# Two heads' scores emptied together: one maximum or one exponential over two PSUM banks

## The chip, the cores and the metric

The kernel runs on one core of a Trainium2 chip. A core has TensorE (matrix products), VectorE and ScalarE (both can read the results of TensorE), GpSimd, and SyncE, which here only issues DMAs. TensorE writes into PSUM: 128 partitions of eight banks, and a bank holds 512 fp32 numbers per partition. Before a bank can be written anew, whoever reads it must have finished.

The metric is the device time of one execution in microseconds. In the profile, PE is TensorE's matrix products, PEld its weight loads (they run beside the products), DVE is VectorE, ACT is ScalarE, POOL is GpSimd and SP is SyncE.

## The reference, cut to what matters

Two layers in a row work on `x` of 2 x 1024 tokens with 256 columns. Each has self-attention with 16 heads of 16 columns, then cross-attention to a context of 64 tokens, then a feed-forward part; in the first layer this is a mixture of eight experts of which each token uses two. The change touches self-attention alone:

```python
q, k, v = heads(q_in, wq, bq), heads(kv_in, wk, bk), heads(kv_in, wv, bv)   # 2 x 16 x 1024 x 16
scores = jnp.einsum('bhqd,bhkd->bhqk', q, k) / jnp.sqrt(jnp.float32(dh))    # 1024 x 1024 per head
attn = jax.nn.softmax(scores, axis=-1)
out = jnp.einsum('bhqk,bhkd->bhqd', attn, v)
```

The softmax needs, for each query, the largest score over 1,024 keys, the exponentials of the scores less that maximum, and their sum.

## The kernel before, in words

All of PSUM is one tile, `banks`, of 128 x 8 x 512. A Python list `free` holds the numbers of the banks that are not promised to anybody, and is worked while the program is written, not while it runs. `bank()` (L260) takes the bank at the head of the list. Whoever takes a bank gives it back to the end of the list as soon as the instruction that empties it has been written down. A bank at the head may therefore still be being read when the program runs; the first matmul that writes it then waits for its reader. Four engines (PE, DVE, ACT, SP) run their instructions in exactly the order in which the code writes them.

Self-attention (`self_attention`, from L556) handles four heads at a time. A *cell* is four heads (j = 0 to 3), 512 queries and 128 keys; a layer has 128 cells, eight to a group of heads. Each cell's scores are computed twice, in two kinds of tiles of 128 x 512, one bank each:

- kind "a", ten cells ahead (`LEAD`): queries in the partitions, 512 keys in the columns. It is two matmuls (the high and low parts of the queries), and VectorE empties it by a maximum over its columns (L911) into `mx`.
- kind "b", for the cell itself: 128 keys in the partitions, 512 queries in the columns. It is three matmuls, of which the third subtracts the maxima (`QB`), and ScalarE empties it by an exponential (L921) into `pt`, a tile of the pool tag "p1" with 12 buffers.

`scores` (L926) writes one cell's tiles. It has four lanes, one per head; a lane uses its own 32 rows of TensorE. In one *wave* each lane writes one matmul. Lanes 0 and 1 have first their "b" tile and then their "a" tile; lanes 2 and 3 the other way round. So waves 1 to 2 finish the "a" tiles of heads 2 and 3, wave 3 the "b" tiles of heads 0 and 1, and wave 5 the other four. Banks are taken at the first wave of a tile: four in wave 1, two in wave 3, two in wave 4. After wave 3, and at the end, the banks of the finished tiles go back to the list, the later finished half and the earlier one in turn (L955). After a full cell the list therefore reads b0 a2 b1 a3 b2 a0 b3 a1, where each bank is named by the tile that it last held.

The main loop (L1100) writes, cell by cell: the scores; at the end of a group `collect` (L968: the maxima over both halves of the keys, laid out for the transposes of `largest`, L804); every second cell, or sometimes for one cell by itself, `product` (L988), which multiplies the exponentials of one or two *earlier* cells by the values (L997, one bank), copies the result out of PSUM on ScalarE (L1006, L1009) and lets GpSimd add it up (L1010); and then a few microseconds of other work which a planner (`Stream`, L141) picks by costs and due times: projections of the next heads (L669: product, split on ScalarE L660 and VectorE L661, DMA), values (L633), cross-attention (L1265, L1304, L1357), and more. All of these take their banks with `bank()`, one or two at a time. The planner's costs don't depend on which banks are free, so the order of the instructions doesn't either. Before the first cell of a layer, ten cells of "a" tiles alone are written (`early`, L959). The last ten cells of a layer hold "b" tiles alone.

The two lines that empty the tiles before:

```python
nc.vector.tensor_reduce(to, sc, AX.X, ALU.max)             # L911: 128 x 512 -> 128 x 1
nc.scalar.activation(pt, sc, AF.Exp, scale=SCALE)          # L921: 128 x 512 -> 128 x 512
```

Of the kernel before, what the change touches and what calls it, by code (L numbers as in the profile page):

```python
# [41 lines left out]
F32 = mybir.dt.float32  # L42
F32R = mybir.dt.float32r
I32 = mybir.dt.int32
U32 = mybir.dt.uint32
AF = mybir.ActivationFunctionType
ALU = mybir.AluOpType
AX = mybir.AxisListType
# [3 lines left out]
P = 128  # L52
# [5 lines left out]
SCALE = 0.25  # L58
# [12 lines left out]
NK = 5  # L71
# [160 lines left out]
def two_blocks(  # L232
# [16 lines left out]
    nc = tc.nc  # L249
# [7 lines left out]
    banks = psum.tile([P, 8, 512], F32, tag="banks", name="banks")  # L257
    free = list(range(8))

    def bank():  # L260


        i = free.pop(0)
        return i, banks[:, i, :]


    x_sb = const.tile([P, NT, D], F32, name="x_sb")
# [41 lines left out]
    ones = const.tile([P, P], F32, name="ones")  # L309
# [236 lines left out]
    def make_heads(pool, layer):  # L546


        KS = [pool.tile([P, S], F32R, name=f"KS{layer}{i}") for i in range(NK)]
        QS = [  # L550
            [pool.tile([P, 512], F32R, name=f"QS{layer}{i}{part}") for part in "hl"]
            for i in range(4)
        ]
        return KS, QS

    def self_attention(layer, tail, heads, arrive, extra, when_ready, beside=None):  # L556
# [6 lines left out]
        names = f"s{layer}"  # L563
        pools = ExitStack()

        def results_pool():
            side = {"side": "right"} if layer else {}
            return tail.enter_context(tc.tile_pool(name=f"opool{layer}", bufs=2, **side))

        def weights_pool():  # L570
            return pools.enter_context(tc.tile_pool(name=f"qpool{layer}", bufs=1, side="right"))
# [7 lines left out]
        if layer == 0:  # L579
            qpool = spool = weights_pool()  # L580
        else:
            spool = pools.enter_context(tc.tile_pool(name="spool", bufs=1))
        KS, QS = heads or make_heads(qpool, layer)
# [14 lines left out]
        QB, mx = {}, {}  # L598
        exps = {}
        now = [-99]  # L600
        reduced = [None]
# [16 lines left out]
        def norm():  # L618
            yield from norm_task(TB, TB, ln, x_turned(1), f"{names}1", held=held[0])
            if layer == 0:  # L620
                add_bias(TB, TB, bias_out[0])
# [166 lines left out]
        def add_heads(b, qh, pair):  # L788
# [3 lines left out]
            if qh == 0:  # L792
                stream.add(
                    keys(b, pair), 3.44, last=last, mark=("K", h),
                    after=[("norm", b)], rank=1,
# [3 lines left out]
        def need_heads(h):  # L799
            if h % 8 in (0, 2) and h > 0:  # L800
                stream.until(("K", h))
            stream.until(("Q", h))
# [92 lines left out]
        def score(kind, cell, j):  # L895

            h, n = divmod(cell, 8)
            b, g = h // 8, h % 4
            K = KS[(4 * b + g) % NK]
            r = slice(32 * j, 32 * j + 32)  # L900
            if kind == "a":
                qc, kh = divmod(n, 2)
                if h not in mx:
                    mx[h] = small.tile([P, 4, 4, 2], F32, tag="mx", name=f"mx_{names}{h}", bufs=3)
                to = mx[h][:, qc, j, kh : kh + 1]
                products = [
                    (q[r, qc * P : (qc + 1) * P], K[r, kh * 512 : (kh + 1) * 512]) for q in QS[h % 4]
                ]

                def reduce(sc):  # L910
                    nc.vector.tensor_reduce(to, sc, AX.X, ALU.max)  # L911
                    return True

                return products, reduce
            products = [(K[r, n * P : (n + 1) * P], q[r, :]) for q in QS[h % 4]]
            r = slice(32 * j, 32 * j + 2)
            products.append((ones[r, :].bitcast(F32R), QB[h][r, :]))

            def drain(sc):
                pt = qpool.tile([P, 512], F32, tag="p1", name=f"pt_{names}{cell}{j}", bufs=12)  # L920
                nc.scalar.activation(pt, sc, AF.Exp, scale=SCALE)  # L921
                exps[cell, j] = pt

            return products, drain

        def scores(lanes):  # L926

            lanes = [[score(*t) for t in lane] for lane in lanes]
            at = [[0, None] for _ in lanes]
            emptied, wave = [], 0  # L930
            while any(lanes):
                done = []
                for lane, now in zip(lanes, at):
                    if not lane:
                        continue
                    products, drain = lane[0]
                    if now[1] is None:
                        now[1] = bank()
                    i, sc = now[1]
                    lhsT, rhs = products[now[0]]  # L940
                    now[0] += 1
                    last = now[0] == len(products)
                    nc.tensor.matmul(sc, lhsT=lhsT, rhs=rhs, start=now[0] == 1, stop=last)  # L943
                    if last:
                        done.append((drain, i, sc))
                        lane.pop(0)
                        now[:] = 0, None
                for drain, i, sc in done:
                    if drain(sc):
                        reduced[0] = i  # L950
                emptied.extend(i for _, i, _ in done)
                wave += 1
                if wave == 3 or not any(lanes):
                    half = len(emptied) // 2
                    for pair in zip(emptied[half:], emptied[:half]):  # L955
                        free.extend(pair)
                    emptied = []

        def early(cell):  # L959

            h, n = divmod(cell, 8)
            if h not in mx:
                mx[h] = small.tile([P, 4, 4, 2], F32, tag="mx", name=f"mx_{names}{h}", bufs=3)
            for c in (cell, cell + 1):
                scores([[("a", c, j)] for j in range(4)])
                yield 0.9

        def collect(h):  # L968
# [87 lines left out]
        else:  # L1056
# [3 lines left out]
            opool, qpool = results_pool(), weights_pool()  # L1060
# [3 lines left out]
        if layer == 1:  # L1064
            stream.made.update([("K", 2), ("Q", 2)])
        for qh, pair in ((0, 1), (1, 0), (1, 1))[layer:]:
# [6 lines left out]
            norm(), 4.0, last=64 - LEAD - 16, mark=("norm", 1), light=True,  # L1073
            after=["measured", ("K", 2), ("Q", 6), ("values", 0, TB - 1)],
        )
# [4 lines left out]
        if layer == 0:  # L1080
# [3 lines left out]
            for ahead in range(0, LEAD, 2):  # L1084
                cell = now[0] = ahead - LEAD
# [14 lines left out]
        for cell in range(ncell + 2):  # L1100
            now[0] = cell
            ahead = cell + LEAD
            if ahead < ncell and ahead % 16 == 0:
                need_heads(ahead // 8)
            has_a, has_b = ahead < ncell, cell < ncell
            maxima[0] = has_a
            lanes = []
            for j in range(4):
                tiles = [("b", cell, j)] * has_b + [("a", ahead, j)] * has_a
                lanes.append(tiles[::-1] if j > 1 else tiles)  # L1110
            scores(lanes)
            if ahead % 8 == 7 and has_a:
                h = ahead // 8
                collect(h)
                stream.add(
                    largest(h), 0.75, first=cell + 1, last=cell + 2, mark=("QB", h), rank=99, light=True
                )
            if (cell + 1) % 8 == 0 and cell + 1 < ncell:
                stream.until(("QB", (cell + 1) // 8))
            for go in later.pop(cell, []):  # L1120
                go()
            if cell >= 2 and cell % 2 == 0:
                product([c for c in (cell - 2, cell - 1) if c not in alone])
            if has_a:
                most = 2.2 - stream.steady(cell, 1.1)
                while cell % 2 == 1 and most > 0.9:
                    cost = stream.step(cell, heavy=True)
                    if cost is None:
                        break
                    most -= cost  # L1130
            else:
                owed = min(owed, 3.0) + max(stream.pace(cell), 2.0)
                if cell % 2 == 0 and owed < 2.5:
                    continue
                most = 2.2
                while owed > 0.5 and most > 0.0:
                    cost = stream.step(cell)
                    if cost is None:
                        break
                    owed -= cost  # L1140
                    most -= cost

            if cell % 2 == 1 and most > 1.2 and cell < ncell:
                alone.add(cell - 1)
                product([cell - 1])
# [989 lines left out]
    def block(layer, tail, heads=None, beside=None):  # L2135
# [75 lines left out]
        def around(*begin):  # L2211
            beside(*begin)
            open_pools()

        stream, later = self_attention(layer, tail, heads, arrive, extra, when_ready, around)
        return stream, later, made, ready

# [12 lines left out]
    stream, later, _, _ = block(0, tail)  # L2230
# [217 lines left out]
```

## Time and profile before

| what | us |
|---|---|
| median of 3 runs | 1542.13 (1539.37 to 1545.07) |
| the profiled execution, its own time | 1547.58 |
| its span, first to last instruction | 1545.8 |
| cells with both kinds of scores, layer 0 | from 66 to 511 |
| the mixture of experts, between the layers | from 511 to 918 |
| cells with both kinds of scores, layer 1 | from 918 to 1345 |
| the last cells and the forward part | from 1345 to 1546 |

Busy time in the stretches that the change touches, and in the whole span (us):

| stretch | PE | PEld | DVE | ACT | POOL |
|---|---|---|---|---|---|
| 66 to 511 | 418.10 | 196.86 | 361.21 | 345.41 | 169.81 |
| 918 to 1345 | 406.65 | 196.62 | 353.08 | 344.74 | 173.16 |
| span | 1444.7 | 840.9 | 1005.8 | 938.7 | 442.7 |

The mean granted clock of TensorE was 0.977. In the page's groups of instructions a row reads: line, engine, operation, output and input, shapes, count; then busy time and the mean length of one in ns; then how long the engine had been idle before them and what ended most of it. In the list of waits a row gives who waited for whom, the total in us, how often, and the longest. In the timeline a row gives start and length in us, engine, line and operation, where neighbouring instructions of one group are merged (x4), and in brackets the idle time before. The chain goes back from the last instruction to whatever released it, piece by piece.

### The profile page before, as it was taken

The page shows a single profiled execution, that of the slowest core. Times are in us where ns is not written, and L with a number is a line of the kernel's source. Part 1 is how long each engine was busy: PE and PEld are TensorE (multiplying, and loading weights), DVE is VectorE, ACT ScalarE, POOL GpSimd, SP SyncE. Part 2 cuts the span into 40 slices and gives each one's busy share as a digit, 9 for nine tenths or more (in the row PEclk, how much of TensorE's full clock was granted, in tenths as well). Part 3 has the DMA queues.
Part 4 walks back from the last instruction along what each step waited for, and adds up shares of the span by engine and source line. Part 5 has one row for each costly group of instructions (what it writes and reads, how often), then busy time and mean ns, then how long its engine had stood idle before and what let it go on. Part 6 is the DMA issues. An engine that isn't in the chain of part 4 may idle for free. (4 is left out here: it accounts for less than half of the span.)

```text
span 1545.8 us, 29995 instructions
## 1 busy us (share of the span) xinstructions
PE 1444.7 (93%) x11220; PEld 840.9 (54%) x11220; DVE 1005.8 (65%) x2219; ACT 938.7 (61%) x1845; POOL 442.7 (29%) x582
## 2 busy tenths in 40 slices
PE   6899999999989987899999999999999999999998
PEld 3443344444445454688888674435444444456666
DVE  6787788889787657541115668977788888844400
ACT  3287787887877834333224347977788788863321
POOL 1142133444553121131112014311265365401010
PEclk9799999999989998999999999999999999999999
DMA  4444641111110021666566542122211112000000
GB/s 158 148 176 162 225 153 49 49 43 36 35 50 15 16 81 41 200 224 235 183 204 234 167 159 76 50 97 76 77 57 35 37 42 80 22 8 29 8 14 27
DMA packets 65605, 146.09 MB, mean 95 GB/s; under 512 B 10570, under 2 KB 24140, under 8 KB 65068
## 3 DMA queue, kind: packets, MB, share of 16 engines
q1 hardware_dynamic: 62236, 135.24, 25.8%
q0 software_dynamic: 3216, 8.85, 1.5%
q8 instruction: 91, 1.49, 0.4%
q14 instruction: 62, 0.51, 0.1%
HBM read 91.96 MB, written 51.86 MB: 93 GB/s over the span
## 5 line engine op out<-in xcount | busy, mean ns | idle before, releaser
L911 DVE TENSOR_REDUCE mx_s<-banks 128x1 f32<-128x512 f32 x1024 | 634.5, 682 | 110.2 <-PE banks L943 109.4
L921 ACT ACTIVATE pt_s<-banks 128x512 f32<-128x512 f32 x1024 | 534.2, 604 | 123.8 <-PE banks L943 117.4
L1010 POOL TENSOR_TENSOR acc_s<-acc_s,part_s 128x512 f32<-128x512 f32 x138 | 176.7, 1281 | 350.3 <-ACT part_s L1009 349.3
L997 PE MATMUL banks<-pt_s,v_s 128*18 128x512 f32 x2048 | 264.5, 611 | 13.1 <-ACT pt_s L921 8.3
L943 PE MATMUL banks<-qb_s,ones 2*128 2x512 f32 x1024 | 203.3, 396 | 0.0
L1947 PE MATMUL banks<-w_slot,h_s 128*128 128x256 f32 x560 | 125.2, 380 | 1.5 <-issue 1.1
L997 PEld LDWEIGHTS banks<-pt_s,v_s 128*18 128x18 f32 x2048 | 42.9, 97 | 132.5 <-ACT pt_s L921 74.7
L1947 PEld LDWEIGHTS banks<-w_slot,h_s 128*128 128x128 f32 x560 | 105.4, 190 | 17.2 <-issue 1.7
L1009 ACT COPY part_s<-banks 128x512 f32<-128x512 f32 x151 | 90.9, 602 | 34.8 <-PE banks L997 33.8
L1956 DVE SCALAR_TENSOR_TENSOR ys<-banks,gate,b 128x256 f32<-128x256 f32 x35 | 16.9, 484 | 136.0 <-PE banks L1947 136.0
L943 PEld LDWEIGHTS banks<-qb_s,ones 2*128 2x128 f32 x1024 | 98.1, 187 | 9.0
L1962 POOL DMA_INDIRECT results<-ys,to x35 | 33.9, 968 | 225.3 <-DVE ys L1956 169.2
L1922 ACT ACTIVATE h_s<-banks,w_slot 128x256 f32<-128x256 f32 (+1 forms) x104 | 41.0, 445 | 92.9 <-issue 53.9
L1916 PE MATMUL banks<-xsT,w_slot 128*128 128x256 f32 (+1 forms) x416 | 85.1, 357 | 0.9 <-ACT xsT L406 0.9
L1916 PEld LDWEIGHTS banks<-xsT,w_slot 128*128 128x128 f32 x416 | 70.9, 190 | 12.0 <-issue 2.8
L2112 PE MATMUL banks<-w_ff,h_f 128*128 128x256 f32 x256 | 57.0, 379 | 0.0
L2103 ACT ACTIVATE h_f<-banks,w_ff 128x512 f32<-128x512 f32 x32 | 21.9, 687 | 56.9 <-PE banks L2100 56.9
L2100 PE MATMUL banks<-hT_f,w_ff 128*128 128x512 f32 x128 | 56.3, 593 | 0.0
L673 PE MATMUL banks<-xT_s,w_att 128*128 128x512 f32 x104 | 51.5, 620 | 2.9 <-ACT pt_s L921 2.2
L1631 POOL DMA_INDIRECT sorted_rows<-xd_m,at_m x32 | 31.2, 976 | 75.4 <-DVE at_m L1623 43.5
L2112 PEld LDWEIGHTS banks<-w_ff,h_f 128*128 128x128 f32 x256 | 48.1, 190 | 7.6 <-issue 1.4
L1922 ACT ACTIVATE h_s<-banks,spare 128x256 f32<-128x256 f32 (+1 forms) x56 | 21.7, 443 | 48.2 <-PE banks L1916 35.6
(371 smaller groups left out, 3064.1 us busy)
## 6 DMA issues: line engine op xcount, KB each, us to landing
w_slot<-in_ff_w_dram SPq DMA_DIRECT2D x40, 576.0 KB
sorted_rows<-fill SPq DMA_DIRECT2D x36, 520.0 KB
w_slot<-in_ff_w_dram SPq DMA_DIRECT2D x26, 514.0 KB
whole<-acc_s SPq DMA_DIRECT2D x30, 256.0 KB
spare<-in_ff_w_dram SPq DMA_DIRECT2D x14, 514.0 KB
q_parts<-spare SPq DMA_DIRECT2D x13, 512.0 KB
KS<-k_parts SPq DMA_DIRECT2D x12, 512.0 KB
k_parts<-spare SPq DMA_DIRECT2D x10, 512.0 KB
```

The lines of the kernel that those rows point to most:

```text
L673: nc.tensor.matmul(p, lhsT=w[:, at + k * D + pair * P : at + k * D + (pair + 1) * P], rhs=xT[b][:, k, blk * 512 : (blk + 1) * 512], start= ...
L911: nc.vector.tensor_reduce(to, sc, AX.X, ALU.max)
L921: nc.scalar.activation(pt, sc, AF.Exp, scale=SCALE)
L943: nc.tensor.matmul(sc, lhsT=lhsT, rhs=rhs, start=now[0] == 1, stop=last)
L997: nc.tensor.matmul(o[32 * j : 32 * j + VW, :], lhsT=V[b][:, cell % 8, 4 * g + j, :], rhs=exps.pop((cell, j)), start=(cell == cells[0]), st ...
L1009: nc.scalar.copy(part, o)
L1010: helper().tensor_tensor(acc[h], acc[h], part, ALU.add)
L1916: nc.tensor.matmul(ph[:, n, :], lhsT=w[:, at : at + P], rhs=xT[:, k, :], start=(k == 0), stop=(k == 1),)
L1922: nc.scalar.activation(h1[:, f, :rows], ph[:, n, :], AF.Gelu, bias=w[:, W_B1 + f : W_B1 + f + 1])
L1947: nc.tensor.matmul(py, lhsT=h1[:, f, h * P : (h + 1) * P], rhs=w[:, f * D : (f + 1) * D], start=(f == 0), stop=(f == 7),)
L2100: nc.tensor.matmul(ph, lhsT=w1[:, at : at + P], rhs=hT[:, k, :], start=(k == 0), stop=(k == 1))
L2112: nc.tensor.matmul(py[:, n, :], lhsT=h1[:, f, t * P : (t + 1) * P], rhs=w2[:, f * D : (f + 1) * D], start=(f == 0), stop=(f == 7),)
```

## The change

Heads 0 and 1 make one pair of lanes, heads 2 and 3 the other. A pair takes two banks at once with the new `two_banks()`: two banks (2k, 2k+1) that lie side by side, both in the list, and among such pairs the one whose later member stands nearest to the head; if there is none, the first two banks of the list. Both tiles of a pair are then emptied by one instruction over 1,024 columns: a maximum of 128 x 2 x 512 into two numbers per partition, or an exponential of 128 x 2 x 512 into one `pt` of 128 x 2 x 512 (six buffers in place of twelve of half the size). Where the two banks do not lie side by side, two instructions are used as before. The order of the matmuls is unchanged. The banks go back to the list pair by pair, after wave 3 and at the end, so that after a full cell the list reads b0 b1 a2 a3 b2 b3 a0 a1.

`bank()`, for all other work, no longer takes simply the head. It looks at the first four of the list and takes the first whose neighbour is not in the list at all, or is among its last three; if there is none, the head.

```diff
--- before.py
+++ after.py
@@ -259,9 +259,19 @@
 
     def bank():
 
-
-        i = free.pop(0)
+        late = free[-3:]
+        i = next((i for i in free[:4] if i ^ 1 not in free or i ^ 1 in late), free[0])
+        free.remove(i)
         return i, banks[:, i, :]
+
+    def two_banks():
+
+        pairs = [(max(map(free.index, (i, i + 1))), i) for i in range(0, 8, 2) if {i, i + 1} <= {*free}]
+        i = min(pairs)[1] if pairs else None
+        got = (i, i + 1) if pairs else free[:2]
+        for i in got:
+            free.remove(i)
+        return [(i, banks[:, i, :]) for i in got]
 
 
     x_sb = const.tile([P, NT, D], F32, name="x_sb")
@@ -895,65 +905,74 @@
         def score(kind, cell, j):
 
             h, n = divmod(cell, 8)
-            b, g = h // 8, h % 4
-            K = KS[(4 * b + g) % NK]
+            g = h % 4
+            K = KS[(4 * (h // 8) + g) % NK]
             r = slice(32 * j, 32 * j + 32)
+            if kind == "a":
+                qc, kh = divmod(n, 2)
+                return [
+                    (q[r, qc * P : (qc + 1) * P], K[r, kh * 512 : (kh + 1) * 512]) for q in QS[h % 4]
+                ]
+            products = [(K[r, n * P : (n + 1) * P], q[r, :]) for q in QS[h % 4]]
+            r = slice(32 * j, 32 * j + 2)
+            return [*products, (ones[r, :].bitcast(F32R), QB[h][r, :])]
+
+        def drain(kind, cell, j, i):
+
+            h, n = divmod(cell, 8)
+            two = i[1] == i[0] + 1
             if kind == "a":
                 qc, kh = divmod(n, 2)
                 if h not in mx:
                     mx[h] = small.tile([P, 4, 4, 2], F32, tag="mx", name=f"mx_{names}{h}", bufs=3)
-                to = mx[h][:, qc, j, kh : kh + 1]
-                products = [
-                    (q[r, qc * P : (qc + 1) * P], K[r, kh * 512 : (kh + 1) * 512]) for q in QS[h % 4]
-                ]
-
-                def reduce(sc):
-                    nc.vector.tensor_reduce(to, sc, AX.X, ALU.max)
-                    return True
-
-                return products, reduce
-            products = [(K[r, n * P : (n + 1) * P], q[r, :]) for q in QS[h % 4]]
-            r = slice(32 * j, 32 * j + 2)
-            products.append((ones[r, :].bitcast(F32R), QB[h][r, :]))
-
-            def drain(sc):
-                pt = qpool.tile([P, 512], F32, tag="p1", name=f"pt_{names}{cell}{j}", bufs=12)
-                nc.scalar.activation(pt, sc, AF.Exp, scale=SCALE)
-                exps[cell, j] = pt
-
-            return products, drain
-
-        def scores(lanes):
-
-            lanes = [[score(*t) for t in lane] for lane in lanes]
-            at = [[0, None] for _ in lanes]
+                to = mx[h][:, qc, j : j + 2, kh]
+                if two:
+                    nc.vector.tensor_reduce(to, banks[:, i[0] : i[0] + 2, :], AX.X, ALU.max)
+                for k in () if two else range(2):
+                    nc.vector.tensor_reduce(to[:, k : k + 1], banks[:, i[k], :], AX.X, ALU.max)
+                reduced[0] = i[1]
+                return
+            pt = qpool.tile([P, 2, 512], F32, tag="p1", name=f"pt_{names}{cell}{j}", bufs=6)
+            if two:
+                nc.scalar.activation(pt, banks[:, i[0] : i[0] + 2, :], AF.Exp, scale=SCALE)
+            for k in () if two else range(2):
+                nc.scalar.activation(pt[:, k, :], banks[:, i[k], :], AF.Exp, scale=SCALE)
+            for k in range(2):
+                exps[cell, j + k] = pt[:, k, :]
+
+        def scores(pairs):
+
+
+            pairs = [list(pair) for pair in pairs]
+            at = [None, None]
             emptied, wave = [], 0
-            while any(lanes):
+            while any(pairs):
                 done = []
-                for lane, now in zip(lanes, at):
-                    if not lane:
+                for p, pair in enumerate(pairs):
+                    if not pair:
                         continue
-                    products, drain = lane[0]
-                    if now[1] is None:
-                        now[1] = bank()
-                    i, sc = now[1]
-                    lhsT, rhs = products[now[0]]
-                    now[0] += 1
-                    last = now[0] == len(products)
-                    nc.tensor.matmul(sc, lhsT=lhsT, rhs=rhs, start=now[0] == 1, stop=last)
-                    if last:
-                        done.append((drain, i, sc))
-                        lane.pop(0)
-                        now[:] = 0, None
-                for drain, i, sc in done:
-                    if drain(sc):
-                        reduced[0] = i
-                emptied.extend(i for _, i, _ in done)
+                    kind, cell = pair[0]
+                    if at[p] is None:
+                        at[p] = two_banks(), [score(kind, cell, 2 * p + k) for k in range(2)]
+                    got, products = at[p]
+                    total = 2 if kind == "a" else 3
+                    n = total - len(products[0])
+                    for (_, sc), left in zip(got, products):
+                        lhsT, rhs = left.pop(0)
+                        nc.tensor.matmul(sc, lhsT=lhsT, rhs=rhs, start=n == 0, stop=n == total - 1)
+                    if n == total - 1:
+                        done.append((kind, cell, 2 * p, [i for i, _ in got]))
+                        pair.pop(0)
+                        at[p] = None
+                for tile in done:
+                    drain(*tile)
+                emptied.extend(tile[3] for tile in done)
                 wave += 1
-                if wave == 3 or not any(lanes):
+                if wave == 3 or not any(pairs):
                     half = len(emptied) // 2
-                    for pair in zip(emptied[half:], emptied[:half]):
-                        free.extend(pair)
+                    for one, other in zip(emptied[half:], emptied[:half]):
+                        free.extend((*one, *other))
+                    free.extend(() if len(emptied) % 2 == 0 else emptied[-1])
                     emptied = []
 
         def early(cell):
@@ -962,7 +981,7 @@
             if h not in mx:
                 mx[h] = small.tile([P, 4, 4, 2], F32, tag="mx", name=f"mx_{names}{h}", bufs=3)
             for c in (cell, cell + 1):
-                scores([[("a", c, j)] for j in range(4)])
+                scores([[("a", c)], [("a", c)]])
                 yield 0.9
 
         def collect(h):
@@ -1104,11 +1123,8 @@
                 need_heads(ahead // 8)
             has_a, has_b = ahead < ncell, cell < ncell
             maxima[0] = has_a
-            lanes = []
-            for j in range(4):
-                tiles = [("b", cell, j)] * has_b + [("a", ahead, j)] * has_a
-                lanes.append(tiles[::-1] if j > 1 else tiles)
-            scores(lanes)
+            tiles = [("b", cell)] * has_b + [("a", ahead)] * has_a
+            scores([tiles, tiles[::-1]])
             if ahead % 8 == 7 and has_a:
                 h = ahead // 8
                 collect(h)
```

## The prediction

> **What bounds the kernel now.** I read the page first (time, engines, groups), then the waits of TensorE's weight loads, then the chain and the timeline of one stretch, and last the timeline cell by cell.
>
> ```profile
> span 1545.8 us, 29995 instructions
> PE 1444.7 (93%) x11220; PEld 840.9 (54%) x11220; DVE 1005.8 (65%) x2219; ACT 938.7 (61%) x1845; POOL 442.7 (29%) x582
> L911 DVE TENSOR_REDUCE mx_s<-banks 128x1 f32<-128x512 f32 x1024 | 634.5, 682 | 110.2 <-PE banks L943 109.4
> L921 ACT ACTIVATE pt_s<-banks 128x512 f32<-128x512 f32 x1024 | 534.2, 604 | 123.8 <-PE banks L943 117.4
> L997 PE MATMUL banks<-pt_s,v_s 128*18 128x512 f32 x2048 | 264.5, 611 | 13.1 <-ACT pt_s L921 8.3
> ```
>
> The changed work is the two largest groups. TensorE looks full at 93%, but its matmul ends are modelled. Its weight loads show the standing still:
>
> ```profile
> PEld banks L943 <- DVE mx_s L911: 124.7, 192, 2.2
> PEld banks L997 <- ACT pt_s L921: 74.7, 151, 3.2
> ```
>
> So bank turnover is on the path. Which drain is waited for, and how much of it, the chain in order of time tells for one cell of layer 1 that holds only scores and one product:
>
> ```profile
> 1108.03 0.94 PE banks L943 x8
> 1109.02 0.61 ACT pt_s L921
> 1109.67 1.05 PE banks L997 x8
> ```
>
> The timeline of the same cell:
>
> ```profile
> 1107.96 0.18 PEld L943 LDWEIGHTS banks<-QS12h,KS 32*128 32x128 f32 x2 [0.85 <-DVE mx_s L911]
> ...
> 1108.74 2.48 DVE L911 TENSOR_REDUCE mx_s<-banks 128x1 f32<-128x512 f32 x4
> ...
> 1109.02 2.06 ACT L921 ACTIVATE pt_s<-banks 128x512 f32<-128x512 f32 x4 [0.28 <-PE banks L943]
> 1109.13 0.40 PE L943 MATMUL banks<-qb_s,ones 2*128 2x512 f32 x2
> 1109.67 0.13 PEld L997 LDWEIGHTS banks<-pt_s,v_s 128*18 128x18 f32 x8 [0.57 <-ACT pt_s L921]
> ...
> 1110.65 0.18 PEld L943 LDWEIGHTS banks<-QS12h,KS 32*128 32x128 f32 x2 [0.85 <-DVE mx_s L911]
> ```
>
> The reader is to see this: four exponentials start at 1109.02, and the product (L997) starts at 1109.67, 0.05 us after the end of the *first* of them (0.61), not after the fourth. It does not need that exponential's result (it multiplies an earlier cell). It needs its bank: before, the free list after a cell's scores reads b0 a2 b1 a3 b2 a0 b3 a1 (named by the tile last held), and the product takes the head, b0's. The cell lasts 1107.96 to 1110.65 = 2.69 us, in three links: 0.57 to the third wave of matmuls, 1.14 from there to the first other matmul (matmul 0.39, hand-over 0.10, exponential 0.61, hand-over 0.04), and 0.98 for the product. VectorE's four maxima (2.48) fit inside.
>
> I then went through the 2 x 118 cells that hold scores of both kinds, in the timeline's rows, and noted the time from the third wave to the first matmul that is not a score: 135 cells lie at 1.13 to 1.2 us (that link), 58 between 1.2 and 1.57 (mean 1.356), 43 above 1.57. In the last two kinds VectorE or a transfer is later than the exponential; 18 cells also enter late, by about 0.35 us, behind a maximum.
>
> **The change, part by part.**
>
> *Pairs instead of tiles on ScalarE.* The rows have no 1,024-column exponential. By columns: the Gelu at L1922 takes 363 ns at 128 columns and 470 at 256, 0.836 ns a column, so 512 more are 0.428 and a pair is 0.597 (median at L921) + 0.428 = 1.025 us. Two single ones, first start to second end, take 1.086 now. These are the two ends, and I take 1.025, since nothing in the rows makes a column dearer in a second bank. ScalarE gets 0.06 us less work a pair, 512 x 0.06 = 31 us of busy time, of which nothing is on the path by itself. But b0's bank now comes free after 1.025 instead of 0.597: 0.43 us later (0.49 at the other end).
>
> *Who waits for that.* After the change the list reads b0 b1 a2 a3 b2 b3 a0 a1. The new `bank()` looks at the first four; the partner of each is free and not among the last three (b3 a0 a1), so it takes the head: b0's bank again. The second single takes b1's. Everything on TensorE's queue behind that first matmul waits too, the next cell's scores included. Per class: 135 cells x 0.43 = 58 us; 58 cells x (1.57 - 1.356) = 12 us; the other 43 cells nothing. Sum +70 us (about +83 with 0.49). Below nothing is excluded here: the pair cannot end before its first half did.
>
> *Pairs on VectorE.* A 32-column maximum (L975) takes 189 ns and a 512-column one 681: 1.025 ns a column, so a pair is 0.681 + 0.525 = 1.206 us against 1.279 for two back to back now. That is 0.073 a pair, 0.146 a cell. It counts only where VectorE sets the pace: the 43 + 18 cells above and the 20 lead-in cells that hold maxima alone, 81 x 0.146 = 12 us. Its ends: nothing, and 256 cells x 0.146 = 37 us if VectorE set the pace everywhere.
>
> The title VectorE: DVE Perf Modes in the Trainium skill, in its section on the fixed extra latency per instruction, gives a read from PSUM 120 fixed cycles on VectorE at 0.96 GHz and 172 on ScalarE at 1.2 GHz. By that rule, 512 instructions fewer on each would be worth 64 and 73 us of engine time, my estimate from that page; the trace says less, because neighbouring instructions already overlap.
>
> *Order of the banks.* The next cell's first wave now takes the pairs a2a3 and b2b3, its third wave a0a1, its fourth the pair that singles broke. Before, the third wave waited for the third maximum and the fourth wave for the fourth; now the third wave waits for both. Its price is between nothing and one maximum (0.60) in the 61 cells that VectorE holds: 37 us. I take nothing: in the cell above the maxima end at 1111.22, and the next third wave would come at 1108.53 + 2.69 + 0.43 = 1111.65. The second pair of exponentials ends 2.05 after the first one's start, at 1111.07; the next first wave would be at 1110.65 + 0.43 = 1111.08: nothing. If that cover goes, it costs its lateness once a cell.
>
> The Trainium skill's Perfetto Trace Analysis, in Matmuls under Optimizing Tensor Performance, wants independent groups to rotate through banks, so that emptying one overlaps filling the next. That speaks against rotating in twos; it states no figure.
>
> *Slack that takes some of it back.* Where VectorE or a transfer is later than the new 1.57 us (43 cells, 21.7 us beyond it) or holds the entry (18 cells, some 6 us), a delay from the cell before is swallowed. Seventeen of the 43 lie at 1.7 behind the projection's split (L660, L661), which itself begins behind the delayed single, and don't swallow it. I take 10 us, between nothing and 28.
>
> *The rest.* Six tiles of two halves hold the same three cells of exponentials as twelve did, and a product reads a cell whole: nothing, and one exponential's wait if a half were kept longer. Matmuls, waves and the planner's order are the same; no DMA moves, so nothing is moved past SP's or POOL's queues. The mixture and the forward part between and after use `bank()` too; a taken bank is at most three places from the head, so at least four uses old: nothing.
>
> Sum: +70 - 12 - 10 = +48 us. The profiled execution took 1547.58 us (its span 1545.8), 5.45 over the median of 1542.13. So 1595.6 by its own time, and **1590** against the median.
>
> **The rivals.**
>
> 1. *The emptying engines set the pace* and shorter instructions win. For it: 124.7 us of weight loads waiting for maxima, and stretches such as this with VectorE unbroken:
>
> ```profile
> 302.47 4.93 DVE L911 TENSOR_REDUCE mx_s<-banks 128x1 f32<-128x512 f32 x8
> ```
>
> Against it: many of those waits are like the 0.85 above, under a product still streaming. It gives 1542 - 37 = 1505. It decides if the first other matmul does not follow the end of the pair.
>
> 2. *The later release is swallowed*: VectorE's cells and the projections' chain take back the full 28 and the product-only cells gain their 12 us, with part of the 58 us falling on cells where the fill was late anyway. Against it: 135 cells at one and the same 1.14 have no slack. About +10: 1552.
>
> 3. *Both releases hurt*: the third wave waits for the second pair of maxima (+37) on top of the dearer pair (+83), and nothing is swallowed but the 12 us: +108, 1650. Against it: 0.43 us of slack in the cell worked above.
>
> **How the numbers follow.** The forecast has 0.72, rival 1 0.12, rival 2 0.08, rival 3 0.08. The forecast's own range is 1565 to 1625 (+23 to +83). For 8 in 10, low goes down to 1545, into rival 2, and high to 1640, most of the way to rival 3; rival 1 is left out. Half a per cent is about what a measurement here can tell: faster 0.11, same 0.05, slower 0.84.
>
> **What would show it.** In the new profile: 512 instructions in each of the two groups, about 1.21 us (VectorE) and 1.03 us (ScalarE). In a cell with one product, 1.57 us from the third wave to the product, which starts 0.05 after the first pair's end, and some 3.12 us for the cell. The weight loads' wait of L997 for pt_s should grow from 74.7 us by roughly the loss, that for mx_s stay or fall. Wrong if ScalarE's pair is far from 1.03 us, if products start before its end, or if the third wave waits for maxima.

## The result, and the profile after

The changed kernel took 1614.35 us (median of four runs, 1608.46 to 1615.43), the kernel before on the same chip 1540.75 us. The ratio is 1.043, with a 95% interval of 1.040 to 1.047. The forecast was slower, 1590 us; the measured time lies within its range and within the likeliest case's own range of 1565 to 1625. The mean granted clock of TensorE was 0.977 in both profiles, so the loss is not one of the clock.

The page of the changed kernel, the lines that answer to those shown of before:

```profile
span 1613.7 us, 28585 instructions
PE 1424.6 (88%) x11220; PEld 818.1 (51%) x11220; DVE 977.9 (61%) x1707; ACT 918.2 (57%) x1333; POOL 442.4 (27%) x582
L930 DVE TENSOR_REDUCE mx_s<-banks 128x2 f32<-128x1024 f32 x512 | 603.0, 1217 | 177.2 <-PE banks L962 129.4
L937 ACT ACTIVATE pt_s<-banks 128x1024 f32<-128x1024 f32 x512 | 501.5, 1022 | 138.1 <-PE banks L962 134.6
L1016 PE MATMUL banks<-pt_s,v_s 128*18 128x512 f32 x2048 | 263.4, 611 | 61.4 <-ACT pt_s L937 59.6
```

The change does what it says. All 1,024 tiles of each kind are emptied in 512 pairs; no pair of banks had to be split. VectorE and ScalarE are busy some 28 and 20 us less than before, and every engine's share of the span has fallen. TensorE has the same 11,220 products, is less busy, and the matmuls of its product L1016 now stand idle 61 us, nearly all of it (59.6) behind exponentials, where those of L997 stood 13 (8.3).

The waits of TensorE's weight loads in the changed kernel (total us, times, longest):

```profile
PEld banks L1016 <- ACT pt_s L937: 124.0, 148, 1.1
PEld banks L962 <- DVE mx_s L930: 63.5, 73, 2.7
```

The wait of the product for an exponential grew from 74.7 to 124.0 us; that of the scores for maxima halved, from 124.7 to 63.5. The same kind of cell that the prediction worked through, scores and one product, now looks like this in the chain:

```profile
1155.12 0.92 PE banks L962 x9
...
1156.06 1.03 ACT pt_s L937
...
1157.14 1.05 PE banks L1016 x8
1158.19 0.91 PE banks L962 x10
...
1159.13 1.03 ACT pt_s L937
```

and in the timeline:

```profile
1155.91 2.36 DVE L930 TENSOR_REDUCE mx_s<-banks 128x2 f32<-128x1024 f32 x2 [0.48 <-ACT part_s L1028]
...
1156.06 1.94 ACT L937 ACTIVATE pt_s<-banks 128x1024 f32<-128x1024 f32 x2 [0.23 <-PE banks L962]
...
1157.14 1.05 PE L1016 MATMUL banks<-pt_s,v_s 128*18 128x512 f32 x8 [0.52 <-ACT pt_s L937]
...
1158.12 0.18 PEld L962 LDWEIGHTS banks<-QS12h,KS 32*128 32x128 f32 x2 [0.85 <-issue]
```

From one pair's start to the next is 1159.13 - 1156.06 = 3.07 us, where the whole cell was 2.69. The product starts 0.05 us after the first pair has ended (1157.09), although it needs nothing of that pair but its bank.

The same accounting over all 2 x 118 cells with both kinds of scores, from the start times of TensorE's rows in the two traces (us):

| | before | after | difference |
|---|---|---|---|
| third wave to the first matmul that is no score, sum | 322.2 | 386.3 | +64.1 |
| of which the 135 cells at 1.13 to 1.2 before | | | +54.0 |
| of which the 58 cells between 1.2 and 1.57 | | | +13.5 |
| of which the 43 cells above | | | -3.5 |
| start of the scores to the third wave, sum | 152.1 | 146.7 | -5.4 |
| the rest of the cells, sum | 400.4 | 397.9 | -2.5 |
| after layer 1's last such cell, to the end | 199.2 | 204.7 | +5.5 |
| everything else (lead-ins, mixture, layer 0's last ten cells) | 471.9 | 478.1 | +6.2 |

### The profile page after: what moved, and what is told of

The parts are those of the page before. It is cut to its first block, busy times and chain, and to the rows that moved or that the text cites. A ratio compares the mean times of both kernels' runs of the same rounds, so it can differ in the third digit from the quotient of the medians.

```text
span 1613.7 us, 28585 instructions
## 1 busy us (share of the span) xinstructions
PE 1424.6 (88%) x11220; PEld 818.1 (51%) x11220; DVE 977.9 (61%) x1707; ACT 918.2 (57%) x1333; POOL 442.4 (27%) x582
## 5 line engine op out<-in xcount | busy, mean ns | idle before, releaser
L930 DVE TENSOR_REDUCE mx_s<-banks 128x2 f32<-128x1024 f32 x512 | 603.0, 1217 | 177.2 <-PE banks L962 129.4
L937 ACT ACTIVATE pt_s<-banks 128x1024 f32<-128x1024 f32 x512 | 501.5, 1022 | 138.1 <-PE banks L962 134.6
L1016 PE MATMUL banks<-pt_s,v_s 128*18 128x512 f32 x2048 | 263.4, 611 | 61.4 <-ACT pt_s L937 59.6
L1016 PEld LDWEIGHTS banks<-pt_s,v_s 128*18 128x18 f32 x2048 | 42.5, 97 | 185.4 <-ACT pt_s L937 124.0
```

The source lines that it names most:

```text
L930: nc.vector.tensor_reduce(to, banks[:, i[0] : i[0] + 2, :], AX.X, ALU.max)
L937: nc.scalar.activation(pt, banks[:, i[0] : i[0] + 2, :], AF.Exp, scale=SCALE)
L1016: nc.tensor.matmul(o[32 * j : 32 * j + VW, :], lhsT=V[b][:, cell % 8, 4 * g + j, :], rhs=exps.pop((cell, j)), start=(cell == cells[0]), st ...
```

## The experiments

All ratios are to the kernel before, run on the same chip beside them. Three chips took part: the kernel before took 1529.08 us on that of the first four experiments, 1528.00 us on that of the next four, and 1541.68 us on that of the last two.

**Which of the parts costs it.** Four kernels take the changed one apart. In the first, the maxima stay paired and each pair of banks is emptied by two exponentials:

```diff
-            if two:
-                nc.scalar.activation(pt, banks[:, i[0] : i[0] + 2, :], AF.Exp, scale=SCALE)
-            for k in () if two else range(2):
+            for k in range(2):
                 nc.scalar.activation(pt[:, k, :], banks[:, i[k], :], AF.Exp, scale=SCALE)
```

> The changed kernel with its pairs of banks and its paired maxima, but each pair emptied by two exponentials of 512 columns, bank b0 first. Release theory (the loss is that the bank of b0 comes free after 1.02 us in place of 0.60, and TensorE's next other matmul waits for it): almost all of the 73 us comes back, 1530 to 1550 us; from the third wave to the first other matmul some 1.14 us again in most cells. Rival, bank order (the third wave waits for all four maxima, and banks go round in twos): nothing comes back but some 10 us, 1600 us or more. Rival, late release of the maxima: 1600 or more too, since the maxima stay paired.

Measured: 1546.84 us, 1.010 (1.007 to 1.014). Most of the loss is gone, but not all: 1% stays. Third wave to first other matmul fell back to a median of 1.157 us.

The second has paired exponentials, and single maxima:

```diff
-                if two:
-                    nc.vector.tensor_reduce(to, banks[:, i[0] : i[0] + 2, :], AX.X, ALU.max)
-                for k in () if two else range(2):
+                for k in range(2):
                     nc.vector.tensor_reduce(to[:, k : k + 1], banks[:, i[k], :], AX.X, ALU.max)
```

> The changed kernel with paired exponentials, but each pair of maxima as two instructions of 512 columns. Release theory: the loss stays, 1610 to 1625 us, and what VectorE's pairs had won (some 0.07 us a pair, where it is on the path) is lost again. Rival, late release of the maxima (the third wave stands behind the pair of maxima): the time comes back to about 1545. Rival, bank order: about 1614, as the release theory, so this run does not tell these two apart.

Measured: 1607.44 us, 1.050 (1.047 to 1.053). The loss stays. With both paired it was 1.043 (1.040 to 1.047, in the first comparison), so the pairs on VectorE are not the cause, and at most a small gain, since the two intervals touch; the rival of late maxima falls.

The third has both of these edits, so that only the choice of banks is left of the change:

> The changed kernel with its new choice of banks alone: every tile emptied by its own instruction of 512 columns. Release theory: about the kernel before, 1535 to 1552 us. Rival, bank order: the loss stays, 1600 or more.

Measured: 1555.82 us, 1.014 (1.010 to 1.018). This is above what the release theory expected (1535 to 1552) and far below what bank order alone as the cause expected. The choice of banks costs something by itself. The fewer and larger `pt` tiles, which this kernel has too, are not it: in its list of waits no exponential waits for a product.

The fourth is the third with the order of the two exponentials turned round:

```diff
-            for k in range(2):
+            for k in (1, 0):
                 nc.scalar.activation(pt[:, k, :], banks[:, i[k], :], AF.Exp, scale=SCALE)
```

> As the run with every tile emptied by itself, but of each two exponentials the one of the odd head first, so that the bank that TensorE's next other work takes comes free after two short exponentials (1.08 us for the two in the profile of before) with no long instruction anywhere. Release theory: the whole loss is back, 1612 to 1630 us, a little more than the changed kernel, since two short ones last 0.06 us longer than a pair. Rival, length of the instruction itself (something in a read over two banks is dear): about 1540, as with every tile by itself in the old order. Rival, bank order: the same as the run with every tile by itself, whatever that is.

Measured: 1626.05 us, 1.062 (1.059 to 1.065). No exponential is longer than in the kernel before (0.601 us on average against 0.604), and the loss is larger than the changed kernel's. The product waits for the second short exponential:

```profile
1173.06 2.07 ACT L935 ACTIVATE pt_s<-banks 128x512 f32<-128x512 f32 x4 [0.26 <-PE banks L958]
...
1174.20 1.91 PE L1012 MATMUL banks<-pt_s,v_s 128*18 128x512 f32 x16 [0.61 <-ACT pt_s L935]
```

The product's start is 1.14 us after the first exponential's, hence at the end of two, and the median from the third wave to the first other matmul is 1.640 us. What costs is the time at which that one bank comes free, not the length of the instruction.

**Where the 1.0 to 1.4% of the bank choice comes from.** The kernel before was profiled once more, on the chip of the second four experiments:

> The kernel before once more, for a profile from the same chip as the experiments. Every theory: some 0.99 to 1.01 of the kernel before; from the third wave to the first other matmul 1.14 us in most cells, few late entries.

Measured: 1528.87 us, span 1527.1. In the cells it agrees with the first profile of before: 323.4, 151.5 and 400.4 us for the three sums of the table, 18 late entries (over 0.7 us from the start of the scores to the third wave). The single-instruction version of the new bank choice has 324.9, 160.1 and 403.4 us, and 50 late entries. One of these late entries in the timeline of the third kernel:

```profile
977.36 2.06 ACT L935 ACTIVATE pt_s<-banks 128x512 f32<-128x512 f32 x4 [0.43 <-PE banks L958]
...
979.00 0.18 PEld L958 LDWEIGHTS banks<-KS,QS13h 32*128 32x128 f32 x1
979.48 0.18 PEld L958 LDWEIGHTS banks<-KS,QS13h 32*128 32x128 f32 x1 [0.30 <-ACT pt_s L935]
```

The fourth lane's first score waits for the last of the four exponentials, which ends at 979.42. Before, a first wave took the banks of a2, b1, a3, b2; with pairs it takes a2, a3, b2, b3, so it stands behind the fourth exponential and not the third. In the changed kernel itself there are only 7 late entries: there the product already starts late by more than that, and the wait is hidden under it. So these two waits do not add.

The entries are only a part of the loss: 8.6 us of the sums above, where the cells together give 13.1 and the medians differ by 27. Ahead of the first cell the third kernel's profile is 10 us longer than the second one of before, at a granted clock of 0.84 against 0.95. That stretch also varies without any change: one of the kernels below (the kernel before with the first maximum's bank first) has the very instructions of the kernel before up to there, and took 5.6 us more, at 0.88.

Whether the rule for *single* banks has a share in it, the next kernel tells: all tiles emptied singly, and `bank()` as it was.

```diff
-        late = free[-3:]
-        i = next((i for i in free[:4] if i ^ 1 not in free or i ^ 1 in late), free[0])
-        free.remove(i)
+        i = free.pop(0)
```

> The changed kernel with every tile emptied by itself, and the old rule for single banks (the head of the list). It tells whether the 1.4% that stayed in the run with the new choice of banks alone lies in the choice of single banks. If it does: 1.00 of the kernel before. If it lies in the banks that the pairs take (the third wave behind all four maxima, the entry behind two of them): 1.01 to 1.02 again.

Measured: 1551.00 us, 1.015 (1.010 to 1.020), 47 late entries. The rule for singles is not it. The late entries come from what the pairs take; but the cells with both kinds of scores are only 7 us longer than in the second profile of before, at nearly the same granted clock (0.977 in layer 0 in both, 0.996 and 0.992 in layer 1), and the medians differ by 23. Where the other 16 come from stays open.

**The same long exponentials, another bank first.** This kernel has paired exponentials and single maxima (1.050), and after wave 3 gives back the pair of maxima first:

```diff
                     half = len(emptied) // 2
+                    if any(pairs):
+                        emptied.reverse()
                     for one, other in zip(emptied[half:], emptied[:half]):
```

> The changed kernel with paired exponentials and single maxima (the run that was 1.050 of the kernel before), and one thing more: after wave 3 the pair of maxima goes back to the list ahead of the pair of exponentials, so that TensorE's next other work takes the bank of a2, free after one short maximum, in place of b0's. Every long exponential stays. Release theory: what counts is when that one bank comes free, some 0.95 us after the third wave; most of the 5.0% comes back, 1.00 to 1.02 of the kernel before. Rival, length of the exponential itself (anything that waits for a pair): 1.04 or more.

Measured: 1556.97 us, 1.019 (1.015 to 1.023). Some 3.1 points of the 5.0 come back by the order of a list alone, with every exponential as long as in the changed kernel. The weight loads of this kernel show what the product waits for now:

```profile
PEld banks L960 <- ACT pt_s L935: 110.2, 142, 3.1
PEld banks L1016 <- DVE mx_s L930: 91.9, 152, 3.0
```

In 94 of the 236 cells the link is at about 1.0 us, shorter than in the kernel before. In the others VectorE is behind. The pair of exponentials is waited for again, but by the next cell's scores.

**The same for the kernel before.** If the first maximum is earlier than the first exponential, the kernel before could gain from this order too:

```diff
                     half = len(emptied) // 2
+                    if any(lanes):
+                        emptied = emptied[half:] + emptied[:half]
                     for pair in zip(emptied[half:], emptied[:half]):
```

> The kernel before, where after wave 3 the list gets a2 b0 a3 b1 in place of b0 a2 b1 a3, so that the next other work takes the bank of the first maximum. Release theory: a2's maximum ends some 0.15 to 0.2 us ahead of b0's exponential where VectorE is not behind; with 119 cells at the 1.14 us link that is 0.98 to 1.00 of the kernel before. Rival (VectorE is behind often enough that its banks are free later): 1.00 to 1.02.

Measured: 1526.99 us, 0.998 (0.9956 to 1.0001). 116 cells have the link at about 1.0 us, but where VectorE is behind it is longer, and the sum falls only from 323.4 to 320.8 us. It is no clear gain.

**Asking for no fresh bank.** Two more kernels write the product of every second cell between the third and the fourth wave, when the head of the list is meant to be a bank emptied a cell ago. In the kernel before:

```diff
+            between = None
+            if cell >= 2 and cell % 2 == 0 and has_a and has_b:
+                between = lambda: product([c for c in (cell - 2, cell - 1) if c not in alone])
-            scores(lanes)
+            scores(lanes, between)
...
-            if cell >= 2 and cell % 2 == 0:
+            if cell >= 2 and cell % 2 == 0 and not (has_a and has_b):
                 product([c for c in (cell - 2, cell - 1) if c not in alone])
```

with `scores` calling `between()` once, after the banks of wave 3 went back to the list.

> The kernel before, where the product of every second cell is written between wave 3 and wave 4 of the cell's scores in place of after them. At that point the head of the list is a bank that was emptied a cell ago, so the product waits for no drain. Release theory: the wait of some 0.3 us (from the end of wave 5 to the end of b0's exponential) goes in up to 118 cells, 0.975 to 0.995 of the kernel before. Rival, VectorE next: the last two maxima of a cell start 1 to 2 us later, the next cell's third and fourth waves stand behind them, and the gain is given back: 1.00 to 1.03.

Measured: 1564.19 us, 1.014 (1.011 to 1.017). Most of the product's wait did go (21.4 us), but the scores wait in its place. The weight loads of this kernel:

```profile
PEld banks L943 <- ACT pt_s L921: 117.5, 231, 1.5
PEld banks L1000 <- ACT pt_s L921: 21.4, 43, 3.4
```

Scores behind exponentials stood at 16.1 us (29 times) before, the product at 74.7. With eight banks and eight score tiles in a cell, whoever comes ninth waits for a drain. The size fits the rival, but its mechanism does not: the wait for maxima did not grow (114.2 us against 124.7).

In the changed kernel, with `bank()` as it was:

> The changed kernel (paired maxima and paired exponentials) with the same move of the product and the old rule for single banks (the head), so that in every second cell no single bank is asked of a pair that was just filled; the other cells keep the wait for the pair. Release theory: about half of the changed kernel's 4.3% comes back, 1.00 to 1.025 of the kernel before. Rival, length of the exponential itself: 1.04 or more.

Measured: 1599.64 us, 1.038 (1.035 to 1.041). At most half a point came back (the changed kernel's 1.043 had the interval 1.040 to 1.047), less than the release theory had it; the rival's 1.04 or more is not clearly met either. This kernel differs from the changed one in two things at once, the place of the product and the rule for singles. In this kernel too the wait has moved: weight loads of the product stand 26.4 us behind exponentials, those of the scores 174.3.

```profile
1132.17 1.94 ACT L935 ACTIVATE pt_s<-banks 128x1024 f32<-128x1024 f32 x2
...
1133.25 0.18 PEld L960 LDWEIGHTS banks<-QS12h,KS 32*128 32x128 f32 x2 [0.81 <-ACT pt_s L935]
...
1134.16 0.42 PEld L407 LDWEIGHTS banks<-ident,xn_c 128*128 128x128 f32 x4 [0.39 <-ACT pt_s L935]
```

The first pair of exponentials from 1132.17 ends at about 1133.2, and the next cell's first scores start at 1133.25; the second ends at 1134.11, and the next single bank starts at 1134.16. The delay is the same two drains, met at other places. Neither of the two beats the kernel before, and none of the other changed kernels clearly does.

## Why the prediction was right

*What the link is.* Right. The prediction read from one cell that the product waits for b0's bank, and for nothing else. The median link went from 1.149 to 1.534 us; the first other matmul starts within 0.02 to 0.08 us of the first exponential instruction's end in 196 of the 236 cells, against 141 before. The turned exponentials (1.062) show it without any long instruction, the turned list (1.050 to 1.019) with all of them.

*The lengths.* 1.022 us for a pair of exponentials (forecast 1.025) and 1.217 for a pair of maxima (forecast 1.206). The column rates of unlike rows (a Gelu at two widths, a maximum at two widths) held.

*Who waits.* The sum by classes was +58, +12 and 0; it was +54.0, +13.5 and -3.5. Per cell of the first class it is 0.40 and not 0.43: in the cell above the pair starts 0.44 us after the third wave (1155.62 to 1156.06) where the single exponential started 0.49 after it, and the medians over the 135 cells are the same two numbers. Why it starts earlier is not shown.

*What takes some of it back* is the step that was mis-sized. The sum took off 12 us for VectorE's pairs and 10 us for swallowed delays. In the cells the late class, the entries and the rest together gave 3.5 + 5.4 + 2.5 = 11.4 us, half of the 22. VectorE's pairs by themselves come to 0.65% with paired exponentials (1.050 to 1.043, two comparisons) and 0.4% with single ones (1.014 to 1.010, one comparison), 6 to 10 us, with intervals as wide as that. If these are right, they are most of what came back, and leave little that was swallowed; the runs do not show the split.

*The order of the banks* was set at nothing inside the changed kernel, with its cover named: the product's delay of 0.43. That held: 7 late entries, and in the cell above the second pair of exponentials ends at 1158.00, 0.12 us before the next scores' first weight load. With the cover gone, the third kernel has 50 late entries and pays 8.6 us for them. The place is the one that the prediction looked at, the next first wave behind the second pair's exponentials; its third rival had looked for the price at the third wave, behind the maxima. That the three kernels without the cover lose 1.0 to 1.5% is more than their cells show (4, 13 and 7 us).

*The rest* was set at nothing and was not: +5.5 us after layer 1's last cell with both kinds, +6.2 elsewhere. The +5.5 look like waits, since this part took 199.2 and 199.1 us in the two profiles of before and 204.7 to 204.9 in the three kernels in which the first bank comes free late. But they go with the granted clock. In the last ten cells, which hold "b" tiles alone:

| kernel | last ten cells, us | TensorE busy, us | granted clock |
|---|---|---|---|
| before, two profiles | 41.3 and 41.4 | 38.2 and 38.3 | 0.96 |
| changed | 45.3 | 41.7 | 0.85 |
| all emptied singly, `bank()` as it was | 41.4 | 40.1 | 0.92 |
| before, product moved | 45.1 | 43.7 | 0.81 |
| pairs, product moved | 39.7 | 36.2 | 1.00 |

TensorE's idle time there grew by only 0.5 us from before to changed; its busy time grew by 3.5, and by 1.6 more in the forward part behind it. Of the kernels with the product moved, the one with every drain short is slow here, and the one with every drain paired is the fastest. (The profile models the ends of matmuls, so the busy times are near values.) What lowers the clock, and whether the change has a share in it, stays open.

Of the +6.2 us elsewhere, 4.8 lie between layer 0's last cell with both kinds and layer 1's first score: 0.9 in layer 0's last ten cells and 3.9 behind them, 320.2 to 324.1 us. In the eight profiles of the two chips of the first eight experiments this last stretch took 304.8 to 305.6 us, and 305.3 in the one of before among them; they show no cost of the change there.

So +48 was forecast and +68 came by the profiled executions (1547.58 to 1615.43; +74 by the medians): the main term was right to 3 us, 11 us too much were taken back, and 12 us lie outside the cells, which the sum did not have. Both of the larger errors made the forecast too low, so that it came out right in its direction and range is not the luck of errors that cancelled.

*The rivals.* That the emptying engines set the pace is refuted: both did less work, and the kernel was slower. That the release is swallowed is refuted by the class sums. That both releases hurt came nearest of the three in time, but not by its mechanism: the scores' wait for maxima fell (124.7 to 63.5 us).

The Trainium skill's Perfetto Trace Analysis asks, in Matmuls under Optimizing Tensor Performance, that independent groups rotate through banks so that emptying overlaps filling. The runs agree and say more than the page: with all eight banks in rotation, it was the time at which the *first* of them comes free that counted, at 0.40 us a cell.

## What to carry to other kernels

Before merging two instructions that empty buffers, look up who takes the first of these buffers next: merging holds it until the last is read, and if somebody stands at that buffer, the loss is the length of the second half each time, here 0.40 us against some 0.06 us of overhead saved. The name in a wait ("product waits for exponential") does not say whether it is for data or for space; the code's order of buffers does, and turning round the order of two equal instructions tests it without any other change. Before a rest of a few us is called a wait, compare TensorE's busy time and granted clock in that stretch: 5 of the 5.5 us at the end of this kernel were busy time. A moved wait is not a removed one: with eight banks for eight tiles, whoever came ninth waited, wherever it was put.

## What the runs showed of the hardware

A maximum or an exponential that reads over two banks costs next to nothing extra: 1.217 and 1.022 us, within 1% of what the column rates of short instructions gave (1.206 and 1.025). Two neighbouring short ones already overlap (1.279 and 1.086 us for two), so that merging them saved 0.062 and 0.064 us a pair.

The Trainium skill's VectorE: DVE Perf Modes, in its section on the fixed extra latency per instruction, gives 120 fixed cycles at 0.96 GHz and 172 at 1.2 GHz for reads from PSUM. As an estimate from that page's figures this is 0.125 and 0.143 us an instruction, twice what a merged pair saved here; the measurement decides.

The kernel before took 1541 us in the first comparison and 1542 beside the last two experiments, but 1529 and 1528 on the two chips of the others. Its two profiles, one from the first comparison and one from a faster chip, have the same cells to within 2 us a layer (446.2 and 428.6 against 445.1 and 430.3). Of the 18.7 us between their spans, 14.9 lie between layer 0's last score and layer 1's first (320.2 against 305.3 us, at a granted clock of 0.968 against 0.983). Why is not shown.

The granted clock also differed by kernel within one stretch: over the last ten cells of layer 1 it was 0.81 to 1.00 in the kernels above.
